# A four-layer float32 block: spectra of small kernels moved to the start, three PSUM banks for attention's first projections, and the scans' weights loaded ahead of a convolution

## The chip, the core and the metric

The kernel runs on one core of one Trainium2 chip, in float32 throughout. The metric is the device time of one execution in microseconds, the median of several runs. The engines are named as the profile names them: PE (TensorE), DVE (VectorE), ACT (ScalarE), POOL (GpSimd), and SP, which here only issues transfers. ACT can issue transfers too, on a queue of its own.

## The reference

The input `x` is an image of 256 x 256 positions with 128 channels (33.5 MB). Four layers follow each other; each one adds to its input a function of the group-normalised input:

```
x = x + L0(_gn(x))   # row attention: layer norm, q, k, v, g = 4 projections of 128 -> 128,
                     # softmax(q k / sqrt(32) + bias) v in 4 heads, per row of 256, gated, projected
x = x + L1(_gn(x))   # 128 -> 2 x 256, depthwise 3x3 convolution, silu, four selective scans
                     # (state 16) along rows and columns, forwards and backwards, gated, projected
x = x + L2(_gn(x))   # truncated Fourier mixing along both axes, then a two-layer MLP
x = x + L3(_gn(x))   # 16 steps of h = f * (A h) + inp, complex, with spectra A and B
```

`_gn` needs mean and variance of its whole input, so no layer can start before the one ahead of it is complete. In L3, A and B are the two-dimensional Fourier transforms, 256 x 256, of 7 x 7 kernels that are inputs of the program; they depend on no layer:

```
def _pad_and_fft(kr, ki, h, w, k):
    kern = kr + 1j * ki
    ph = (h - k) // 2
    pw = (w - k) // 2
    padded = jnp.pad(kern, ((0, 0), (ph, h - k - ph), (pw, w - k - pw)))
    return jnp.fft.fft2(padded, axes=(-2, -1))
```

In L1 the scans need, besides the convolution's output, four small weights: `x_proj_w`, `dt_w` with its bias, exp of `A_logs`, and `Ds`.

## The kernel before, in words

The image is kept as 128 channels (partitions) by 65536 positions and goes through DRAM between the stages: `x` to `x1` (layer 0), `x2p` and `x2` (layer 1), `x3` (layer 2), `out` (layer 3). `program()` at L1640 calls them in turn.

**Statistics.** `stream_stats` (L76) reads `x` in 32 loads of 1 MB, issued by SP into four buffers `xs_t`, and DVE makes `bn_stats` of four pieces of 512 positions of each. `group_norm_coef` (L52 to L72) then makes the scale and shift `ab` of the normalisation: `bn_aggr` (L60), two small matmuls, a square root on ACT (L70), a reciprocal. Later layers make their statistics while they write their outputs.

**Layer 0.** `layer0` loads `w_q` to `w_o`; `row_norm` (L102) loads three more constants and makes a layer norm in 32 blocks of 2048 positions: load x (`l0a_x`, four buffers), centre by a matmul (L141), square, variance by matmul, root, reciprocal, spread by matmul, scale, affine; it writes `z` and a bias of four rows. `attention` (L231) then goes through 32 blocks of 8 rows. A block needs 16 projections (`project`, L265): four pieces of 512 positions times k, q, v, g. Each is one matmul (four small ones for v, L272; else L277) into the PSUM tile `l0b_mm`, of which there is one buffer, and one evacuation out of it, by DVE for k and v (L275, L279), by ACT for q and g (L281, L283). The 16 projections of block 0 come first, before anything else is there to do; those of every later block are mixed into the units of the block before it. A unit is half a row's heads: scores (L291) with a running bias (L302), exponentials (L317), a division on POOL (L326), transposes into the two PSUM tiles `l0b_tp0` and `l0b_tp1`, the product with v, a gate, and an output projection once per two rows (also through `l0b_mm`).[...]

**Layer 1.** `conv_block` (L414) loads `l1a_win` and `l1a_taps` and multiplies them (L436), then goes through 16 blocks of 16 image rows and two halves of the 256 inner channels: x1 loaded (`l1a_xp`, L453), normalised on DVE (L457), projected (`l1a_pi`, L466), copied by ACT into `l1a_xi` (L473), the nine taps divided between PE, ACT, POOL and DVE, and a silu that writes both `l1a_o` and its transposed sibling `l1a_ot` (L530), stored to `l_xc` (L535, 1 MB) and `l_xct` (L539, 4 MB). Then `scan_weights` (L915) loads `xproj`, `dtw`, `alog` and `ds` on SP, makes exp of `alog` (L922), multiplies it by −1 (L923), and makes four diagonal matrices `dsum` out of the sum of `ds` (L926, L930). `scan_stream` goes through 4 directions of 128 chunks of 512 positions. A chunk's way is: block load `l1b_xc` (L641), xproj matmuls into `l1b_du` (L665), a copy to `l1b_xd` (L677), a store and broadcast loads of B and C (L679 to L691), the softplus of dt (L697 to L731), `l1b_du` and `l1b_db` (L739, L761), and per state the exponential `l1b_da` (L779) and the scan itself (L794) on DVE. `scan_end` merges the four directions.

**Layer 2** works through Fourier matrices on PE. **Layer 3** (`layer3`, L1383) begins with `kernel_spectra` (L1350): three loads, 8 accumulated pairs of matmuls (L1368 to L1372; the profile counts two instructions for each float32 matmul, 32), 32 evacuations into `l3k_o` on DVE (L1374 to L1377), and two stores of 1.79 MB into the DRAM tile `l_spec`. It then scales its weights (`wall`, `ball`, L1408 to L1416), loads a block of x (`l_x`) and 4 rows of `spec` (`l_tu`), makes the second half of the transform (`l_sps`, L1453) and the gates (`l_gp`, L1481), and runs the 16 steps on the whole block.

**What sets the order.** Within `row_norm`, `attention`, `conv_block`, `scan_stream` and `scan_end` the order of the instructions of each engine is written out by hand (`manual_schedule`); in layer 3 this holds for ACT alone. Elsewhere, and between these parts, the scheduler of the tile framework orders them by its own costs. Each engine, SP and ACT's queue included, carries out its stream in that order, and a wait at its head holds all behind it. SBUF comes from pools, which take over the room of pools that were closed before; the tile that is written there first waits for the last readers of what lay there.

Of the kernel before, what the change touches and what calls it, by code (L numbers as in the profile page):

```python
# [10 lines left out]
F32 = mybir.dt.float32  # L11
AF = mybir.ActivationFunctionType
ALU = mybir.AluOpType
AX = mybir.AxisListType
PSUM = bass.MemoryType.PSUM
DRAM = bass.MemoryType.DRAM

P = 128
S = 256
NPOS = S * S  # L20
CH = 512
# [21 lines left out]
        self.pool = pool  # L43


def load(nc, pool, src, name):
    to = pool.tile(list(src.shape), F32, name=name)
    nc.sync.dma_start(to, src)
    return to


# [179 lines left out]
def attention(c, x, x1, zs, bs, w, stats):  # L231
# [3 lines left out]
    tc, nc = c.tc, c.nc  # L235
# [4 lines left out]
    with ExitStack() as a:  # L240
        one = a.enter_context(tc.tile_pool(name="l0b_one", bufs=1))
        io = a.enter_context(tc.tile_pool(name="l0b_io", bufs=2))
        wk = a.enter_context(tc.tile_pool(name="l0b_wk", bufs=2))
        ps2 = a.enter_context(tc.tile_pool(name="l0b_p2", bufs=2, space=PSUM))
        ps1 = a.enter_context(tc.tile_pool(name="l0b_p1", bufs=1, space=PSUM))
# [19 lines left out]
        def project(b, i):  # L265
            k = blocks[b]
            j, n = i // 4, "kqvg"[i % 4]
            cs = bass.ts(j, CH)
            mm = ps1.tile([P, CH], F32, name="l0b_mm")
            if n == "v":  # L270
                for m in range(4):
                    nc.tensor.matmul(  # L272
                        mm[:, bass.ts(m, P)], k["z"][:, bass.ts(4 * j + m, P)], w["v"], start=True, stop=True
                    )
                nc.vector.tensor_copy(k["v"][:, 4 * j : 4 * j + 4].rearrange("p m o -> p (m o)"), mm)  # L275
                return
            nc.tensor.matmul(mm, w[n], k["z"][:, cs], start=True, stop=True)  # L277
            if n == "k":
                nc.vector.tensor_copy(k["k"][:, cs], mm)  # L279
            elif n == "q":  # L280
                nc.scalar.activation(k["q"][:, cs], mm, AF.Copy, scale=float(1.0 / np.sqrt(32)))  # L281
            else:
                nc.scalar.activation(k["g"][:, cs], mm, AF.Tanh, scale=0.5)  # L283
# [44 lines left out]
        def transposes(u):  # L328
            e = es.pop(u)
            for kt in range(2):  # L330
                tp = ps1.tile([P, 2, 2, P], F32, name=f"l0b_tp{kt}")
                for h in range(2):
                    for jt in range(2):
                        nc.tensor.transpose(tp[:, h, jt], e[:, 2 * h + jt, bass.ts(kt, P)], c.ident)
                at = ats[u, kt] = wk.tile([P, 2, S], F32, name=f"l0b_at{kt}")
                if kt == 0:
                    nc.scalar.copy(at, tp.rearrange("p h j q -> p h (j q)"))
                else:
                    nc.vector.tensor_copy(at, tp.rearrange("p h j q -> p h (j q)"))
# [44 lines left out]
        for i in range(UB):  # L384
            project(0, i)
# [3 lines left out]
        for u in range(N + 3):  # L389
            b, i = divmod(u, UB)  # L390
# [521 lines left out]
        y_out(N - 1, 1)  # L912


def scan_weights(c, pool):  # L915
    nc, t = c.nc, c.t
    w = {
        "xproj": load(nc, pool, t["l1_xproj"], "l1_xproj"),
        "dt": load(nc, pool, t["l1_dtw"], "l1_dtw"),
        "A": load(nc, pool, t["l1_alog"], "l1_A"),  # L920
    }
    nc.scalar.activation(w["A"], w["A"], AF.Exp)  # L922
    nc.vector.tensor_scalar(w["A"], w["A"], -1.0, None, ALU.mult)  # L923
    ds_ = load(nc, pool, t["l1_ds"], "l1_ds")
    both = pool.tile([P, 2, 2], F32, name="l1_both")
    nc.vector.tensor_tensor(both, ds_[:, 0:2], ds_[:, 2:4], ALU.add)  # L926
    w["dsum"] = pool.tile([P, 2, 2, P], F32, name="l1_dsum")
    for k in range(2):
        for dh in range(2):
            nc.vector.tensor_scalar(w["dsum"][:, k, dh], c.ident, both[:, k, dh : dh + 1], None, ALU.mult)  # L930
    return w


def scan_end(c, x1, ab, y02, y13, x2p, x2, stats):
# [412 lines left out]

def kernel_spectra(c, dram_t):  # L1350


    tc, nc, t = c.tc, c.nc, c.t
    with ExitStack() as a:
        one = a.enter_context(tc.tile_pool(name="l3k_one", bufs=1))
        wk = a.enter_context(tc.tile_pool(name="l3k_wk", bufs=2))
        ps = a.enter_context(tc.tile_pool(name="l3k_ps", bufs=2, space=PSUM))
# [3 lines left out]
        for ut in range(2):  # L1361
            us = bass.ts(ut, P)

            o = wk.tile([P, 2, 7, 2, 2, 64], F32, name="l3k_o")
            for q0, nq in ((0, 4), (4, 3)):
                qs = slice(q0, q0 + nq)
                re = ps.tile([P, nq, 2, 64], F32, name="l3k_re")
                nc.tensor.matmul(re, phase[:, 0, us], kr[:, qs], start=True, stop=False)  # L1368
                nc.tensor.matmul(re, phase[:, 1, us], ki[:, qs], start=False, stop=True)
                im = ps.tile([P, nq, 2, 64], F32, name="l3k_im")  # L1370
                nc.tensor.matmul(im, phase[:, 0, us], ki[:, qs], start=True, stop=False)
                nc.tensor.matmul(im, phase[:, 2, us], kr[:, qs], start=False, stop=True)  # L1372
                for ab_ in range(2):
# [4 lines left out]
            nc.sync.dma_start(  # L1378
                dram_t[us].rearrange("u r f -> u (r f)"), o.rearrange("u s q k r c -> u (s q k r c)")
            )  # L1380


def layer3(c, x3, out, ab):  # L1383

# [3 lines left out]
    tc, nc, t = c.tc, c.nc, c.t  # L1388
# [2 lines left out]
    NB = NPOS // BL  # L1391
    full, half = [P, NT, 2, 64], [P, NT, 64]
    with ExitStack() as a:
        dram = a.enter_context(tc.tile_pool(name="l3_dram", bufs=1, space=DRAM))
# [25 lines left out]
        phase = load(nc, one, t["c_phase_w"], "l3_phase")  # L1420
# [324 lines left out]
```

## Time and profile before

| what | us |
|---|---|
| runs of the kernel before: lowest, median, highest | 34311.81, 34312.65, 34319.6 |
| profiled execution, its own time | 34318.44 |
| its span in the trace | 34316.7 |
| first statistics (loads and bn_stats) | 7.7 to 87.6 |
| row norm, from the first centre matmul | 96.92 to about 545 |
| attention: projections of block 0 | 558.33 to 602.64 |
| attention, all | to 2919 |
| convolution, from its first load to the last store issued | 2926.5 to 3889.8 |
| scans: first wait for weights to the end of the last chunk | 3889.8 to about 29520 |
| merging of scans; layer 2 | to about 30600; to 32117 |
| layer 3 | 32117 to 34316.7 |

The times of the stages are read off the timeline of the profiled execution, in microseconds from the start of its span. Over the whole span PE is busy 85%, DVE 91%, ACT 66% and POOL 80%, and the mean clock granted to PE is 0.917 of the full one. A line of a timeline gives start, duration, engine, line and operation, output and input tiles, and in brackets the idle time just before it with what ended that. A line of the windows view gives, for a stretch of the span, the busy time and the number of instructions of each engine, the granted clock, the share of the 16 transfer engines that was busy, and the rate in GB/s.

### The profile page before, as it was taken

How to read it: one execution, taken by the hardware profiler on the slowest of the kernel's cores; microseconds unless marked ns; L12 is line 12 of the kernel's file. 1: busy time of each engine (PE TensorE's matmuls, PEld its weight loads, DVE VectorE, ACT ScalarE, POOL GpSimd, SP SyncE). 2: the span in 40 equal slices, each digit the busy share in tenths (PEclk: the TensorE clock that was granted, in tenths of full speed). 3: DMA queues.
4: the chain of work that ended last, by engine and by line, in shares of the span. 5: the costliest groups of instructions: out<-in, count | busy, mean ns of one | idle time of the engine just before them, and what ended most of it. 6: DMA issues, size and time to landing. Idle time of an engine off the chain costs nothing. (4 is left out here: it accounts for less than half of the span.)

```text
span 34316.7 us, 256885 instructions
## 1 busy us (share of the span) xinstructions
PE 29098.7 (85%) x72308; PEld 12172.7 (35%) x72308; DVE 31152.4 (91%) x23833; ACT 22759.1 (66%) x46957; POOL 27431.3 (80%) x6996
## 2 busy tenths in 40 slices
PE   7999888888888888888888888888888888899888
PEld 2554333333333333333333333333333333334444
DVE  5668999999999999999999999999999999863699
ACT  3667777777777777777677777777777777532476
POOL 2446799999999999999999999999999999620000
PEclk8999999999999999999999999999999999999888
DMA  3113455555555555555555555555555555674111
GB/s 137 45 42 119 186 190 191 189 191 192 191 190 191 191 190 191 191 191 189 196 201 203 201 202 199 202 201 202 201 201 200 201 202 203 211 235 144 64 34 33
DMA packets 2076531, 5947.89 MB, mean 173 GB/s; under 512 B 115207, under 2 KB 1379608, under 8 KB 1499222
## 3 DMA queue, kind: packets, MB, share of 16 engines
q1 hardware_dynamic: 1939926, 5864.32, 47.3%
q10 hardware_dynamic: 135168, 67.13, 0.7%
q8 instruction: 570, 9.34, 0.1%
q14 instruction: 867, 7.10, 0.1%
HBM read 5238.41 MB, written 692.58 MB: 173 GB/s over the span
## 5 line engine op out<-in xcount | busy, mean ns | idle before, releaser
L794 DVE TENSOR_TENSOR_SCAN l1b_h<-l1b_da,l1b_state,l1b_db 128x1024 f32<-128x1024 f32 x8192 | 18793.6, 2336 | 596.2 <-ACT l1b_db L783 585.3
L809 POOL TENSOR_TENSOR l1b_hc<-l1b_h,l1b_cc 128x2048 f32<-128x2048 f32 x4096 | 18444.4, 4527 | 329.9 <-DVE l1b_h L794 329.9
L828 PE MATMUL l1b_y<-l1b_hc,ident 128*128 128x512 f32 x32768 | 16054.5, 639 | 1108.4 <-POOL l1b_hc L809 1108.4
L779 ACT ACTIVATE l1b_da<-l1b_dl,l_A 128x512 f32<-128x512 f32 (+1 forms) x16384 | 11297.4, 690 | 3156.0 <-DVE l1b_h L794 2848.1
L828 PEld LDWEIGHTS l1b_y<-l1b_hc,ident 128*128 128x128 f32 x32768 | 6526.4, 205 | 10680.7 <-issue 8160.1
L761 POOL TENSOR_TENSOR l1b_db<-l1b_bb,l1b_dus 128x2048 f32<-128x2048 f32 x1536 | 6965.0, 4535 | 46.9 <-DMA l1b_bb<-l1b_bc 46.9
L761 DVE TENSOR_TENSOR l1b_db<-l1b_bb,l1b_du 128x2048 f32<-128x2048 f32 x2048 | 4658.6, 2275 | 35.2
L783 ACT ACTIVATE l1b_db<-l1b_state,l1b_db,l1b_af 128x1 f32<-128x1 f32 x8192 | 3045.1, 372 | 0.0
L697 PE MATMUL l1b_mm<-l1b_xd,l_dtw 41*128 41x512 f32 x2048 | 1373.4, 755 | 1694.3 <-ACT l1b_dus L750 1688.5
L723 PE MATMUL l1b_mm<-l1b_tail,ident 128*128 128x512 f32 x2048 | 1296.2, 719 | 1399.8 <-ACT l1b_tail L717 1397.3
L805 ACT COPY l1b_state<-l1b_h 128x4 f32<-128x4 f32 x4095 | 789.6, 193 | 2433.5 <-DVE l1b_h L794 2433.4
L326 POOL TENSOR_TENSOR l0b_e<-l0b_e,l0b_den 128x1024 f32<-128x1024 f32 x512 | 969.0, 1893 | 1403.2 <-DVE l0b_den L325 784.3
L723 PE MATMUL l1b_mm<-l1b_relu,ident 128*128 128x512 f32 x2048 | 1313.9, 730 | 0.0
L697 PEld LDWEIGHTS l1b_mm<-l1b_xd,l_dtw 41*128 41x128 f32 x2048 | 338.4, 206 | 2508.9 <-ACT l1b_dus L750 2111.6
L750 ACT COPY l1b_dus<-l1b_mm 128x512 f32<-128x512 f32 x512 | 299.6, 585 | 1388.6 <-DVE l1b_db L761 1388.1
L761 DVE TENSOR_TENSOR l1b_db<-l1b_bb,l1b_mm 128x2048 f32<-128x2048 f32 x512 | 1171.6, 2288 | 18.2 <-ACT l1b_dus L750 0.7
L302 DVE CUSTOM_DVE_ANT_0 l0b_e<-l0b_sc,l0b_bias 128x256 f32<-128x256 f32 x2048 | 745.4, 420 | 419.3 <-PE l0b_sc L291 416.0
L723 PEld LDWEIGHTS l1b_mm<-l1b_tail,ident 128*128 128x128 f32 x2048 | 376.8, 207 | 2070.6 <-ACT l1b_tail L717 1822.7
L317 ACT ACTIVATE l0b_e<-l0b_e,l0b_top 128x256 f32<-128x256 f32 x2048 | 1012.1, 498 | 1.9 <-DVE l0b_top L302 1.9
L665 PE MATMUL l1b_du<-l1b_xc,l_xproj 128*40 128x512 f32 x2048 | 981.6, 602 | 32.7 <-DMA l_xproj<-in_l_xproj 29.1
L731 ACT COPY l1b_dl<-l1b_mm 128x512 f32<-128x512 f32 x1024 | 587.4, 574 | 524.6 <-DVE l1b_du L739 517.2
L985 POOL TENSOR_TENSOR l1c_y<-l1c_y,l1c_yt 128x512 f32<-128x512 f32 x256 | 394.7, 1564 | 606.6 <-DMA l1c_y<-l_y 527.1
(261 smaller groups left out, 30140.8 us busy)
## 6 DMA issues: line engine op xcount, KB each, us to landing
l1b_bb<-l1b_bc SPq DMA_DIRECT2D x2048, 1024.0 KB
l1b_cc<-l1b_bc SPq DMA_DIRECT2D x2048, 1024.0 KB
l1b_xc<-l_xc SPq DMA_DIRECT2D x128, 1024.0 KB
l_y<-l1b_yo SPq DMA_DIRECT2D x128, 1024.0 KB
l1b_xc<-l_xct SPq DMA_DIRECT2D x256, 512.0 KB
l_y<-l1b_yo SPq DMA_DIRECT2D x256, 512.0 KB
l_xc<-l1a_o SPq DMA_DIRECT2D x64, 1024.0 KB
l_xct<-l1a_ot SPq DMA_DIRECT2D x16, 4096.0 KB
```

The costliest lines, as they stand in the source:

```text
L317: nc.scalar.activation(e[:, i], e[:, i], AF.Exp, scale=-1.0, bias=top[:, i : i + 1], accum_out=den[:, i : i + 1],)
L326: nc.gpsimd.tensor_tensor(e, e, den[:, :, None].to_broadcast([P, 4, S]), ALU.mult)
L665: nc.tensor.matmul(du1[:40], w["xproj"][:, dh, k, :], in_block(blocks[ch][0], ch, dh), start=dh == 0, stop=dh == 1,)
L697: nc.tensor.matmul(mm, w["dt"][:, chunks[ch][0], dh * P : dh * P + P], xds[ch % 3][0:41], start=True, stop=True,)
L723: nc.tensor.matmul(mm, c.ident, part, start=i == 0, stop=i == 1)
L761: eng.tensor_tensor(db, bbs[g // 2], du[:, None, :].to_broadcast([P, G, CH]), ALU.mult)
L779: nc.scalar.activation(da[:, o + lo : o + hi], dl[:, lo:hi], AF.Exp, scale=w["A"][:, k, dh, n : n + 1])
L783: nc.scalar.activation(first, states[k][:, dh, two : two + 1], AF.Identity, scale=af[:, two : two + 1], bias=first,)
L794: nc.vector.tensor_tensor_scan(h_, a_, d_, states[k][:, dh, one : one + 1], ALU.mult, ALU.add)
L805: nc.scalar.copy(states[k][:, dh, n0 : n0 + G], hs[g][:, :, 0 if k >= 2 else CH - 1])
L809: nc.gpsimd.tensor_tensor(hc, hs[g], ccs[g // 2], ALU.mult)
L828: nc.tensor.matmul(ys[j % 2], c.ident, hc[:, i], start=False, stop=j // 2 * G + i == 15)
```

## The change

There are three parts.

First, `kernel_spectra` is called in `program()` ahead of `stream_stats`, within one group of pools that is closed after both. Its three loads and its two stores are issued by ACT instead of SP, its 32 evacuations are made by ACT instead of DVE, and `spec` is a DRAM tile of the program.

Second, the 16 projections of attention's block 0 take in turn the PSUM tiles `l0b_mm`, `l0b_tp0` and `l0b_tp1`. The later blocks use `l0b_mm` as before. The transposes' tiles have their shape changed to suit both.

Third, the four weights of the scans are loaded before `conv_block` is called, issued by ACT; `scan_weights` keeps the arithmetic, and its place in the program's text.

In the built program the streams of the engines differ as follows. PE: the spectra's 16 matmuls stand at its start. ACT: three loads, 32 copies and two stores at its start; and, after the square root of layer 1's coefficients, the four weight loads, the table load and the exponential of `alog`, all ahead of the first copy into `l1a_xi`. DVE: the 32 copies are gone from layer 3, and the arithmetic on `ds` and on the exponential stands ahead of the multiplication of the taps. SP: the three loads and two stores of the spectra and the four weight loads are gone; two loads of x for the statistics wait for the completion of the two `spec` stores, since completions are counted on eight shared lanes; the row norm's first two loads of x stand ahead of `w_q` to `w_o`; at the convolution's start the two loads of `l1a_xp` wait for `xproj` and `dtw` on such lanes; and at its end the last stores of `l_xc` and `l_xct` stand ahead of the first two loads of `l1b_xc`, behind which they stood before. All other instructions keep their order on their engines.

```
-def load(nc, pool, src, name):
+def load(nc, pool, src, name, queue=None):
     to = pool.tile(list(src.shape), F32, name=name)
-    nc.sync.dma_start(to, src)
+    (queue or nc.sync).dma_start(to, src)
...
-            mm = ps1.tile([P, CH], F32, name="l0b_mm")
+            bank = ("mm", "tp0", "tp1")[i % 3] if b == 0 else "mm"
+            mm = ps1.tile([P, CH], F32, name=f"l0b_{bank}")
...
-                tp = ps1.tile([P, 2, 2, P], F32, name=f"l0b_tp{kt}")
+                tp = ps1.tile([P, CH], F32, name=f"l0b_tp{kt}")
+                tp = tp.rearrange("p (h j q) -> p h j q", h=2, j=2)
...
-def scan_weights(c, pool):
-    nc, t = c.nc, c.t
-    w = {
-        "xproj": load(nc, pool, t["l1_xproj"], "l1_xproj"),
-        "dt": load(nc, pool, t["l1_dtw"], "l1_dtw"),
-        "A": load(nc, pool, t["l1_alog"], "l1_A"),
-    }
+def scan_weights(c, pool, w):
+    nc = c.nc
+    w["A"], w["dt"], ds_ = w["alog"], w["dtw"], w["ds"]
     nc.scalar.activation(w["A"], w["A"], AF.Exp)
     nc.vector.tensor_scalar(w["A"], w["A"], -1.0, None, ALU.mult)
-    ds_ = load(nc, pool, t["l1_ds"], "l1_ds")
...
-        conv_block(c, x1, ab, xc, xct)
         with tc.tile_pool(name="l1_w", bufs=1) as wp:
+            w = {n: load(c.nc, wp, c.t[f"l1_{n}"], f"l1_{n}", c.nc.scalar) for n in ("xproj", "dtw", "alog", "ds")}
+            conv_block(c, x1, ab, xc, xct)
             tc.keep_in_program_order(c.nc.scalar.preload_act_table_set(EXP_LN))
-            w = scan_weights(c, wp)
+            scan_weights(c, wp, w)
...
-        kr = load(nc, one, t["l3_kr"], "l3k_kr")
-        ki = load(nc, one, t["l3_ki"], "l3k_ki")
-        phase = load(nc, one, t["c_phase_h"], "l3k_phase")
+    kr = load(nc, one, t["l3_kr"], "l3k_kr", nc.scalar)
+    ki = load(nc, one, t["l3_ki"], "l3k_ki", nc.scalar)
+    phase = load(nc, one, t["c_phase_h"], "l3k_phase", nc.scalar)
...
-                    nc.vector.tensor_copy(o[:, 0, qs, ab_, 0], re[:, :, ab_])
-                    nc.vector.tensor_copy(o[:, 0, qs, ab_, 1], im[:, :, ab_])
-                    nc.vector.tensor_copy(o[:, 1, qs, ab_, 0], im[:, :, ab_])
-                    nc.vector.tensor_scalar(o[:, 1, qs, ab_, 1], re[:, :, ab_], -1.0, None, ALU.mult)
-            nc.sync.dma_start(
+                nc.scalar.copy(o[:, 0, qs, ab_, 0], re[:, :, ab_])
+                nc.scalar.copy(o[:, 0, qs, ab_, 1], im[:, :, ab_])
+                nc.scalar.copy(o[:, 1, qs, ab_, 0], im[:, :, ab_])
+                nc.scalar.mul(o[:, 1, qs, ab_, 1], re[:, :, ab_], -1.0)
+        nc.scalar.dma_start(
...
-        spec = dram.tile([S, 14, 256], F32, name="l3_spec")
-        kernel_spectra(c, spec)
...
-        stream_stats(c, t["x"], c.stats[0])
+        spec = dram.tile([S, 14, 256], F32, name="l3_spec")
+        with ExitStack() as a:
+            kernel_spectra(c, spec, a)
+            stream_stats(c, t["x"], c.stats[0])
...
-        layer3(c, x3, out, group_norm_coef(c, c.stats[1], "3"))
+        layer3(c, x3, out, spec, group_norm_coef(c, c.stats[1], "3"))
```

More of the change, by code (lines that the diff above doesn't have):

```diff
@@ L930, in scan_weights @@
             nc.vector.tensor_scalar(w["dsum"][:, k, dh], c.ident, both[:, k, dh : dh + 1], None, ALU.mult)
-    return w
 def scan_end(c, x1, ab, y02, y13, x2p, x2, stats):
@@ L1344, in layer2, with kernel_spectra @@
                 nc.sync.dma_start(x3[:, sl], xo)
-def kernel_spectra(c, dram_t):
+def kernel_spectra(c, dram_t, a):
     tc, nc, t = c.tc, c.nc, c.t
[L1354 to L1357, printed above, removed]
-        kr = load(nc, one, t["l3_kr"], "l3k_kr")
-        ki = load(nc, one, t["l3_ki"], "l3k_ki")
-        phase = load(nc, one, t["c_phase_h"], "l3k_phase")
[L1361 to L1373, printed above, removed]
-                    nc.vector.tensor_copy(o[:, 0, qs, ab_, 0], re[:, :, ab_])
-                    nc.vector.tensor_copy(o[:, 0, qs, ab_, 1], im[:, :, ab_])
-                    nc.vector.tensor_copy(o[:, 1, qs, ab_, 0], im[:, :, ab_])
-                    nc.vector.tensor_scalar(o[:, 1, qs, ab_, 1], re[:, :, ab_], -1.0, None, ALU.mult)
-            nc.sync.dma_start(
-                dram_t[us].rearrange("u r f -> u (r f)"), o.rearrange("u s q k r c -> u (s q k r c)")
-            )
@@ L1383, in layer3 @@
-def layer3(c, x3, out, ab):
+    one = a.enter_context(tc.tile_pool(name="l3k_one", bufs=1))
+    wk = a.enter_context(tc.tile_pool(name="l3k_wk", bufs=2))
+    ps = a.enter_context(tc.tile_pool(name="l3k_ps", bufs=2, space=PSUM))
+    kr = load(nc, one, t["l3_kr"], "l3k_kr", nc.scalar)
+    ki = load(nc, one, t["l3_ki"], "l3k_ki", nc.scalar)
+    phase = load(nc, one, t["c_phase_h"], "l3k_phase", nc.scalar)
+    for ut in range(2):
+        us = bass.ts(ut, P)
+        o = wk.tile([P, 2, 7, 2, 2, 64], F32, name="l3k_o")
+        for q0, nq in ((0, 4), (4, 3)):
+            qs = slice(q0, q0 + nq)
+            re = ps.tile([P, nq, 2, 64], F32, name="l3k_re")
+            nc.tensor.matmul(re, phase[:, 0, us], kr[:, qs], start=True, stop=False)
+            nc.tensor.matmul(re, phase[:, 1, us], ki[:, qs], start=False, stop=True)
+            im = ps.tile([P, nq, 2, 64], F32, name="l3k_im")
+            nc.tensor.matmul(im, phase[:, 0, us], ki[:, qs], start=True, stop=False)
+            nc.tensor.matmul(im, phase[:, 2, us], kr[:, qs], start=False, stop=True)
+            for ab_ in range(2):
+                nc.scalar.copy(o[:, 0, qs, ab_, 0], re[:, :, ab_])
[3 more added lines that the diff above has]
+        nc.scalar.dma_start(
+            dram_t[us].rearrange("u r f -> u (r f)"), o.rearrange("u s q k r c -> u (s q k r c)")
+        )
@@ L1388, in layer3 @@
+def layer3(c, x3, out, spec, ab):
     tc, nc, t = c.tc, c.nc, c.t
@@ L1393, in layer3 @@
     with ExitStack() as a:
-        dram = a.enter_context(tc.tile_pool(name="l3_dram", bufs=1, space=DRAM))
         one = a.enter_context(tc.tile_pool(name="l3_one", bufs=1))
-        spec = dram.tile([S, 14, 256], F32, name="l3_spec")
-        kernel_spectra(c, spec)
         io = a.enter_context(tc.tile_pool(name="l3_io", bufs=3))
```

## The prediction

> **What bounds the kernel now.** I read the page's groups first, for the resource that sets the time, then the windows of the four places that the edits touch, then the timeline and the chain of waits there. The columns of a timeline line are start, duration, instruction, and in brackets the idle time before it and what ended it.
>
> ```profile
> L794 DVE TENSOR_TENSOR_SCAN l1b_h<-l1b_da,l1b_state,l1b_db 128x1024 f32<-128x1024 f32 x8192 | 18793.6, 2336 | 596.2 <-ACT l1b_db L783 585.3
> ```
> VectorE's scans are 18793.6 us of a span of 34316.7 and run from 3943 to about 29520 us. No edit touches their loop, so all that can change lies in what stands once, in series, ahead of them and after them: shares of some tens of us.
>
> ```profile
> 10.00:80.00 70.00, 0.00 (x0) 0.00 (x0) 69.30 (x113) 0.00 (x0) 0.00 (x0) 1.00 1.01 421
> 84.00:88.00 4.00, 0.00 (x0) 0.00 (x0) 3.96 (x7) 1.28 (x1) 0.00 (x0) 1.00 0.01 4
> 558.33:602.64 44.31, 33.10 (x57) 13.09 (x57) 5.54 (x8) 5.46 (x8) 0.00 (x0) 0.50 0.15 60
> 3905.00:3911.00 6.00, 3.23 (x4) 0.38 (x2) 0.00 (x0) 0.00 (x0) 0.00 (x0) 0.50 0.06 23
> 32128.70:32154.10 25.40, 24.21 (x32) 10.29 (x32) 10.28 (x32) 0.00 (x0) 0.00 (x0) 0.50 0.17 72
> ```
> Columns: busy time of PE, weight load, DVE, ACT, POOL, then granted clock, DMA share, GB/s. First statistics: transfers (1.01) and VectorE (69.30 of 70) are both full, and the transfers are done by 84. Projections: TensorE busy 33.1 of 44.3 us at half clock. Start of the scans: nothing but a transfer at 23 GB/s. Spectra: TensorE alone, at half clock.
>
> ```profile
> 597.12 0.60 ACT L281 ACTIVATE l0b_q<-l0b_mm 128x512 f32<-128x512 f32 x1 [5.02 <-PE l0b_mm L277]
> 597.77 2.07 PE L272 MATMUL l0b_mm<-l_wv,l0b_z 128*128 128x128 f32 x8 [0.69 <-ACT l0b_q L281]
> 599.88 0.69 DVE L275 COPY l0b_v<-l0b_mm 128x512 f32<-128x512 f32 x1 [4.93 <-PE l0b_mm L272]
> 600.63 2.08 PE L277 MATMUL l0b_mm<-l0b_z,l_wg 128*128 128x512 f32 x2 [0.79 <-DVE l0b_v L275]
> ...
> 3889.79 0.33 SPq L539 DMA_DIRECT2D l_xct<-l1a_ot  x1
> 3904.63 3.61 PE L665 MATMUL l1b_du<-l1b_xc,l_xproj 128*40 128x512 f32 x4 [29.08 <-DMA l_xproj<-in_l_xproj]
> 3911.03 0.31 ACT L922 ACTIVATE l_A<-l_A 128x128 f32<-128x128 f32 x1 [19.96 <-DMA l_A<-in_l_alog]
> 3911.24 0.56 ACT L677 COPY l1b_xd<-l1b_du 40x512 f32<-40x512 f32 x1
> ```
> Matmul and evacuation alternate through the one bank `l0b_mm`; the scans' first chunk waits for two weight loads that were issued behind a 4 MB store of `l_xct`.
>
> ```profile
> 32128.68 2.04 PE l3k_re L1368 x2
> ...
> 32154.12 5.70 DMA l_spec<-l3k_o
> 32160.02 3.88 DMA l_x<-x
> ```
> The chain in layer 3 runs through the spectra's matmuls (32 records), a store and the first x load behind it.
>
> [...]a pass over 512 columns takes 0.856 us cold, 0.43 warm; the conv warmed 4.8 us after its first matmul (2939.11 to 2943.9), the row norm after 3.7.[...] `dtw` has 41 rows[...]; its 168 KB between 3905 and 3911 are the 0.06 share and 23 GB/s above.[...]
>
> **A. Spectra beside the statistics, what it adds.** Two stores of `spec`, 1.79 MB each, and three small loads: 3.67 MB, at the best rate seen (434 GB/s, 8 to 10 us) 8.45 us, in a stage whose transfers are full. Slack: VectorE needs the last block at 85.06 and it landed at 84.0, 1.1 us; VectorE is faster than a block's transfer by 0.08 us (2.497 us against 2.58 at 406 GB/s), some 2 us over the rest of the stage. So the statistics end 8.45 − 1.1 − 2 = about 5.1 us later than 87.56. The 16 matmuls and 32 evacuations cost nothing: TensorE and ScalarE are idle in this window. SP, two of whose loads wait until the stores have landed (completion lanes are shared), may add to that; four buffers of 2.5 us cover it. Back again: the row norm's first matmul, at 96.92, had waited 2.64 us for its x load; in the changed order two x loads stand ahead of the weights and are there by 90. Net **+2.5 us**; bounds −2.5 (all hidden) and +5.
>
> **B. Projections over three banks.** Sixteen in 44.31 us, 2.77 each, are matmul 2.07, evacuation 0.60 to 0.69 and two handoffs. With three banks the evacuation of one lies beside the next matmuls, and TensorE runs without a gap: 2 × 0.856 = 1.71 us each cold, 16 × 1.71 = 27.4; that is the floor of the gain, 16.9 us. [...]after some 5 us cold (three projections) 13 × 0.856 = 11.1, sum 16.2, a gain of 28.1. Evacuations at 0.6 to 0.69 alternate over two engines, so they keep up with 0.856. Then the scores start warm, where before the clock stayed at half until 622.85; that stretch holds 17.2 us of PE work, but it is a fill in which each step waits on other engines (PE busy 17.2 of 20.2), and it may go cold again. I take 3.5 of a possible 1 to 6. **−31.6 us**; bounds −17 and −35. The tp banks are first used for transposes after scores that follow the last projection, so nothing new waits there.
>
> **C. Weights loaded ahead of the convolution, what it adds.** In the new order ScalarE's stream has the four DMAs, the table load and exp(`alog`) ahead of its first `l1a_xi` copies, and VectorE's has the products of `ds` and −exp(A) ahead of the multiplication of the taps (L436, 2.56 us at 2934.07) and the two normalisations of the conv's input (1.35 and 1.61 us). Both engines work in order, so the conv's start waits for `alog` to land. `alog` shares the queue with `dtw`, which took 6 us alone on one engine and here meets the taps and x loads: I put its landing at 2940, from 2936.5 (alone) to 2942. After it: exp 0.31, ×−1 0.23, dsum 0.88, taps 2.56, and the two normalisations 2.96: the second ends at about 2947.3 where it ended at 2942.6. ScalarE's copies wait no longer than the matmuls do, and TensorE's cold stretch comes as much later. That is 4.7 us, and about 1.1 for the taps' own transfer, which shares the engines with four more: **+5.8 us**; bounds +1 and +10.
>
> **D. Start of the scans, what it removes.** The waits for `xproj` (3904.63) and `alog` (3911.03) go. What is late next: in the new order SP issues the last `l_xct` store (4 MB, issue 3889.79) ahead of the scans' first `l1b_xc` load, which stood before it, at 3876.74. The store's data run until about 3902.6 (`xproj`, queued behind it, landed at 3904.6), then 1 MB at the 300 GB/s of such loads is 3.4 us: 3906, and the copy of `l1b_xd` at 3906 + 1.75 + 0.5 = 3908.3 instead of 3911.24. **−2.9 us**; bounds −6 and 0. Had the load kept its place, the whole 15 us would have gone.
>
> **E. Layer 3, what it removes.** `l_ball` is there at 32124.5. Before: `l_sps`, which opens the loop, began at 32166.08. After: three loads fewer and no store on SP, so x is issued at about 32126.8 and with its 3.88 us is there at 32130.7; the shift's matmuls and the scaled weights (32131.0) and two gp matmuls (2.05) put `l_sps` at 32133.1. **−32.9 us**; bounds −30 and −36. The store of `spec` is long done.
>
> **Sum.** 2.5 − 31.6 + 5.8 − 2.9 − 32.9 = −59.1. The profiled execution took 34318.44 us (span 34316.7), which gives 34259.3; it stands 5.8 above the median of the runs, 34312.65, from which the forecast is 34312.65 − 59.1 = 34253.5, **34254**. This is 0.17%. I take 0.2% (68.6 us: 34244 and 34381) as about what a measurement of this kernel can tell from no change.
>
> **Rivals.**
> 1. Everything hides: statistics −2 (the x loads' head start counts, the stores don't), projections −35, conv +1, scans −6, layer 3 −36: −78, 34235; with one or two of these only, some 34240. For it: four x buffers, three free engines. Against: a DMA share of 1.01, and VectorE's new order. Chance of passing −68.6: 0.2.
> 2. The clock stays cold in the projections (−17), or the conv waits for its upper bound (+10): −40 to −45, about 34270. For it: TensorE stayed at half clock for 44 us with a busy share of 75%. Chance 0.16.
> 3. Slower:[...] Its centre matmuls come at 146.55, 160.20, 173.86, 187.51, a period of 13.65[...].[...] Against: [...]the three runs agree within 8 us. Chance 0.02.
> 4. The weights' early load brings nothing (the 4 MB store decides): it is the sum's D at 0 with C at +5.8, and lies in the forecast's range, 34257.
>
> **Numbers.** Forecast with rival 4: 0.62; rivals 1, 2, 3: 0.2, 0.16, 0.02. The range goes from rival 1's single parts, 34238, to rival 2 with both, 34276. Faster by over 0.2%: 0.2; within: 0.79; slower: 0.01.
>
> **What would show it.** A: the last bn_stats ends near 92.7, the first centre matmul is near 99.4. B: projections in about 16 us with the clock at 1.00 from the third or fourth on; 27 us and 0.50 would be rival 2. C: the taps' multiplication on VectorE waits for `l_A`, and the first `l1a_xi` copy comes near 2948 after allowing for A and B. D: the first `l1b_du` matmul waits for `l1b_xc`, no weight. E: `l_sps` 9 us after `ab`. Wrong would be a new wait inside the scans or the attention's steady state: nothing is moved there, so each would have to keep its length to within some us.

## The result, and the profile after

The changed kernel takes 34256.26 us (median of 20 runs, 34247.13 to 34261.2) where the kernel before takes 34312.65 (20 runs beside it, 34299.25 to 34319.6): 56.4 us less, a ratio of 0.9984 with a 95% interval of [0.9978, 0.999]. The forecast was 34254. The profiled execution of the changed kernel has a span of 34249.9, that of before 34316.7, so the two traces are 66.8 apart, 10 more than the medians; where those 10 come from is told below the table.

Each row is a stretch between two marks that both traces have; the third column of numbers is the difference.

| stretch, from mark to mark | before | after | difference | forecast |
|---|---|---|---|---|
| start to bn_aggr (L60): first statistics | 87.60 | 97.88 | +10.3 | +5.1 |
| to the first centre matmul (L141) | 9.32 | 6.72 | −2.6 | −2.6 |
| row norm, to the first projection | 461.41 | 462.23 | +0.8 | 0 |
| 16 projections, to the first scores | 44.31 | 16.74 | −27.6 | −28.1 |
| attention, to layer 1's square root (L70) | 2323.37 | 2320.48 | −2.9 | −3.5 |
| to the first copy into `l1a_xi`, then to the last silu | 963.76 | 968.64 | +4.9 | +5.8 |
| to the first scan | 53.38 | 50.34 | −3.0 | −2.9 |
| all scans, to the first step of their merging | 25604.47 | 25605.12 | +0.7 | 0 |
| merging, to layer 2's square root | 1058.25 | 1045.37 | −12.9 | 0 |
| layer 2, to layer 3's square root | 1517.45 | 1516.99 | −0.5 | 0 |
| to the first `l_sps` | 42.69 | 9.41 | −33.3 | −32.9 |
| rest of layer 3 | 2150.69 | 2149.98 | −0.7 | 0 |

The stretches that the change touches come to −54.2, close to the −56.4 of the medians. Of the +4.9 of the convolution, 4.1 lie at its start, up to the first copy into `l1a_xi` (16.75 to 20.88 us after the square root); the rest is spread over 948 us and is not told from chance. The 12.9 of the merging belong to no edit: its instructions and their order are the same in both kernels, and in the profiles of the twelve runs below and of these two it took from 1039.7 to 1058.3 us, the kernel before at the upper end. One profile against one profile would have credited the change with it.

The windows view of the kernel after; the stretches answer to those shown of before (first statistics in two parts, projections, the scores' start, start of the scans, layer 3's way to `l_sps`):

```profile
10.00:50.00 40.00, 18.45 (x26) 7.97 (x24) 28.63 (x49) 9.43 (x31) 0.00 (x0) 1.00 1.01 408
50.00:90.00 40.00, 0.00 (x0) 0.00 (x0) 39.66 (x65) 0.00 (x0) 0.00 (x0) 1.00 1.01 420
566.83:583.57 16.74, 16.74 (x57) 9.62 (x57) 5.53 (x8) 5.46 (x8) 0.00 (x0) 0.84 0.36 148
583.57:603.78 20.21, 15.66 (x107) 10.19 (x106) 12.11 (x58) 13.67 (x48) 8.44 (x5) 0.83 0.00 0
3885.00:3889.00 4.00, 0.00 (x0) 0.00 (x0) 0.00 (x0) 0.00 (x0) 0.00 (x0) 0.50 0.85 321
32091.16:32099.99 8.83, 3.91 (x5) 0.69 (x5) 1.99 (x7) 0.91 (x1) 0.00 (x0) 0.50 0.67 202
```

In the 40 us of the first line VectorE is busy 28.63 instead of nearly all, though the transfers stay full: that is the loss. (The clock's 1.00 in the first two lines means nothing: the trace has no record of the clock before 108 us, and the spectra's matmuls over 512 columns follow each other at 0.85 us, as those in layer 3 of the kernel before do at 0.50.) In the projections TensorE is busy 16.74 of 16.74, and the mean clock of 0.84 says that some 5 us were cold (0.5) and the rest warm. The scans' start still waits for a transfer, now at 321 GB/s: a large one, not the 23 GB/s of `dtw`.

VectorE's timeline in the first statistics of the kernel after:

```profile
7.24 12.46 DVE L83 BATCH_NORM_STATS2 stats<-xs_t 128x6 f32<-128x512 f32 x20 [6.25 <-DMA xs_t<-in_x]
28.53 0.09 DVE L119 MEMSET l_wb<- 128x32 f32 x1 [8.84 <-PE l3k_im L1369]
28.53 9.55 DVE L83 BATCH_NORM_STATS2 stats<-xs_t 128x6 f32<-128x512 f32 x16
39.52 7.46 DVE L83 BATCH_NORM_STATS2 stats<-xs_t 128x6 f32<-128x512 f32 x12 [1.44 <-DMA xs_t<-in_x]
47.96 49.89 DVE L83 BATCH_NORM_STATS2 stats<-xs_t 128x6 f32<-128x512 f32 x80 [0.97 <-DMA xs_t<-in_x]
```

Three idle times, 11.25 us together. The longest stands ahead of a clearing of `l_wb`, a tile of the row norm that lies in the spectra's room and so waits for their last matmul.

The timeline at the start of the convolution, at the start of the scans, and the chain in layer 3, of the kernel after:

```profile
2917.27 0.31 ACT L920 ACTIVATE l_alog<-l_alog 128x128 f32<-128x128 f32 x1 [9.88 <-DMA l_alog<-in_l_alog]
2918.88 2.55 DVE L438 TENSOR_TENSOR l1a_taps<-l1a_taps,l1a_win 128x2304 f32<-128x2304 f32 x1
2924.93 0.58 ACT L475 COPY l1a_xi<-l1a_pi 128x512 f32<-128x512 f32 x1 [7.34 <-PE l1a_pi L468]
...
3872.71 0.32 SPq L541 DMA_DIRECT2D l_xct<-l1a_ot  x1
3873.20 2.43 SPq L643 DMA_DIRECT2D l1b_xc<-l_xc  x2
3889.83 3.61 PE L667 MATMUL l1b_du<-l1b_xc,l_xproj 128*40 128x512 f32 x4 [31.37 <-DMA l1b_xc<-l_xc]
```
```profile
32093.85 3.96 DMA l_x<-x
...
32099.99 7.12 PE l_sps L1447 x16
```

This is as forecast: VectorE multiplies the taps only after the weights' arithmetic; the first matmul of the scans waits for `l1b_xc`, which is issued 0.5 us behind the 4 MB store; in layer 3 only the load of x is left.

### The profile page after: what moved, and what is told of

Its sections match the earlier page's. It is cut to its first block, busy times and chain, and to the rows that moved or that the text cites. A ratio compares the mean times of both kernels' runs of the same rounds, so it can differ in the third digit from the quotient of the medians.

```text
span 34249.9 us, 256893 instructions
## 1 busy us (share of the span) xinstructions
PE 29062.3 (85%) x72308; PEld 12164.1 (36%) x72308; DVE 31137.1 (91%) x23801; ACT 22770.2 (66%) x46991; POOL 27433.4 (80%) x6996
## 5 line engine op out<-in xcount | busy, mean ns | idle before, releaser
L781 ACT ACTIVATE l1b_da<-l1b_dl,l_alog 128x512 f32<-128x512 f32 (+1 forms) x16384 | 11297.5, 690 | 3156.6 <-DVE l1b_h L796 2848.7
```

What stands on the lines that cost most here:

```text
L781: nc.scalar.activation(da[:, o + lo : o + hi], dl[:, lo:hi], AF.Exp, scale=w["A"][:, k, dh, n : n + 1])
```

## The experiments

Medians are given as the difference to the runs of the kernel before that were made beside them: 34314.04 for `p1_spectra`, `p2_banks`, `p3_weights` and `two_banks`, 34311.88 for `a_memset`, `c_late`, `d_room` and `all_three`, 34307.52 for `s_stall`, `s_late`, `c_split` and `best`. The interval of such a ratio is about ±0.0008 of it, ±27 us; so the totals tell the parts of the change from each other only roughly, and the stretches of the profiles decide.

**The three parts alone.** `p1_spectra`, the kernel before with the spectra moved only:

```
+            kernel_spectra(c, spec, a)
             stream_stats(c, t["x"], c.stats[0])
```

> The kernel before with the first part alone (spectra beside the statistics). Theory, part by part sum: statistics end near 97.9 as in the changed kernel, first centre matmul +7.7, layer 3's way from its coefficients to the first l_sps −33; together −25, about 34287. Rival, that layer 3's saving is partly given back later because its first blocks arrive before ACT is ready: −15 or less, over 34297.

−26.8 us (34287.28; 0.9992 [0.9984, 1.0]). bn_aggr at 97.84, first centre matmul at 104.55, `l_sps` 9.44 after the square root. The rest of layer 3 takes 2150.5 us, as before, so nothing of the saving is given back there.

`p2_banks`, the kernel before with the banks only:

```
+            bank = ("mm", "tp0", "tp1")[i % 3] if b == 0 else "mm"
+            mm = ps1.tile([P, CH], F32, name=f"l0b_{bank}")
```

> The kernel before with the second part alone (three banks for the first projections). Theory: projections 16.7 us instead of 44.3 with the clock at full from the third on, the attention's rest 2.9 shorter since it starts warm; −30.5, about 34282. Rival[...]: projections near 27 us, −17, about 34296.

−32.7 us (34281.33; 0.9991 [0.9983, 0.9999]). The window of its projections:

```profile
558.95:575.98 17.03, 17.03 (x56) 9.62 (x57) 5.54 (x8) 5.46 (x8) 0.00 (x0) 0.82 0.38 156
```

The same picture at another time in the run, so the warm clock is no accident. In all ten profiles with three banks the projections took 16.7 to 17.0 us, in the three with one bank 44.3 each time.

`p3_weights`, the kernel before with the weights' loads moved only:

```
+            w = {n: load(c.nc, wp, c.t[f"l1_{n}"], f"l1_{n}", c.nc.scalar) for n in ("xproj", "dtw", "alog", "ds")}
             conv_block(c, x1, ab, xc, xct)
```

> The kernel before with the third part alone (weights loaded ahead of the convolution). Theory: the convolution's first part is 4.9 us later, the scans' start 3.0 earlier: +1.9, about 34314, not to be told from before. Rival, that the early load of weights is worth its whole wait of 15 us: −10, about 34303.

+2.1 us (34316.12; 1.0 [0.9992, 1.0009]), no difference. The first copy into `l1a_xi` comes 21.58 us after the square root instead of 16.75, the first scan 50.1 after the last silu instead of 53.4. The three parts come to −57.4, the whole change to −56.4: as far as totals with such intervals can tell, they add up. The third part's two stretches, +4.8 and −3.2, leave nothing that can be seen.

**How many banks.** `two_banks`, the changed kernel:

```
-            bank = ("mm", "tp0", "tp1")[i % 3] if b == 0 else "mm"
+            bank = ("mm", "tp0")[i % 2] if b == 0 else "mm"
```

> The changed kernel with two banks instead of three for the first projections. Theory[...]: a bank's turn is 1.02 + 0.69 + two handoffs of 0.1 = 1.9 us for two projections, so 0.95 each against 0.87: the projections take about 18 us at full clock, 34258. Rival (the third bank is needed to warm): projections over 25 us at half clock, 34265 or more.

Projections 17.83 us, −52.5 in all (34261.55). Three lines of its timeline, two turns of TensorE and an evacuation beside them, and the window of the scores' start:

```profile
578.17 1.02 PE L278 MATMUL l0b_tp<-l0b_z,l_wq 128*128 128x512 f32 x2
578.37 0.69 DVE L280 COPY l0b_k<-l0b_mm 128x512 f32<-128x512 f32 x1 [1.22 <-PE l0b_mm L278]
579.12 1.16 PE L273 MATMUL l0b_mm<-l_wv,l0b_z 128*128 128x128 f32 x8
```
```profile
584.92:605.13 20.21, 16.22 (x89) 10.23 (x88) 10.07 (x48) 12.31 (x44) 7.54 (x4) 0.66 0.00 0
```

One overlap is what matters: in the projections the second bank gives 26.5 of the 27.6 us, the third the remaining 1.1, since a bank's turn of matmul, evacuation and handoffs (1.9 us, in which two projections are made) is a little longer than two warm matmuls (2 × 0.86 us). In the scores' start, which follows, the one profile with two banks is colder (0.66 instead of 0.83), and its attention takes 2322.8 us, only 0.6 less than before.

**The statistics' delay.** `a_memset`, the changed kernel with `l_wb` in room of its own:

```
-        wb = one.tile([P, 32], F32, name="l0_wb")
-        nc.vector.memset(wb, 0.0)
+        wb = c.wb
```

`c.wb` is a tile of the shared pool that is cleared at the start.

> The changed kernel with l0_wb in room of its own and cleared at the start, so that VectorE's clearing of it no longer waits for the spectra's last matmul. Theory (of the 10.3 us by which the statistics end later, the spectra's 3.7 MB of transfers make 5 to 7, VectorE's 8.84 us wait the rest): bn_aggr starts near 93 to 95 instead of 97.9, 34252. Rival (transfers alone set the end, VectorE only waits somewhere else): 97 to 98, 34256.

bn_aggr at 96.61, only 1.3 earlier; −55.1 in all (34256.81). The theory of two causes that add up fell. VectorE's timeline of this run:

```profile
7.09 14.91 DVE L85 BATCH_NORM_STATS2 stats<-xs_t 128x6 f32<-128x512 f32 x24 [6.06 <-DMA xs_t<-in_x]
24.00 2.47 DVE L85 BATCH_NORM_STATS2 stats<-xs_t 128x6 f32<-128x512 f32 x4 [1.99 <-DMA xs_t<-in_x]
29.88 4.93 DVE L85 BATCH_NORM_STATS2 stats<-xs_t 128x6 f32<-128x512 f32 x8 [3.41 <-DMA xs_t<-in_x]
...
46.79 49.71 DVE L85 BATCH_NORM_STATS2 stats<-xs_t 128x6 f32<-128x512 f32 x80 [0.32 <-DMA xs_t<-in_x]
```

The one wait for a matmul has become five waits for transfers (two of them, 1.64 and 2.59 us, are left out here), 9.95 us in all instead of 11.25. One rival is that SP's order costs the time, not the bytes: SP waited 3.2 us in this run for a store of `l_spec` to land before it issued a load of x. But in every window of 5 us from 5 to 95 us the transfers' share was 0.99 or more, so there was nothing left to be won by issuing earlier. To see each cause without the other, the stores were taken out of the stage: `s_stall`, and with `l_wb` moved too, `s_late`:

```
             stream_stats(c, t["x"], c.stats[0])
+            for there, o in os_:
+                c.nc.sync.dma_start(there, o)
```

> As the run with the late stores, but l0_wb lies in the spectra's room as in the change, so VectorE's clearing still waits for the spectra's last matmul. Theory (in the changed kernel that wait of 8.8 us lay over the wait for transfers, which is why its removal alone gave 1.3): with the stores gone it is bare, bn_aggr starts near 96. Rival (the clearing's wait is made of the transfers' delay and goes with it): below 90.

> The changed kernel with the two stores of the spectra issued by SP behind the last load of the statistics, and l0_wb in room of its own, cleared at the start. Theory (VectorE is at 99% in this stage, so each wait for a transfer is lost for good, and the stores' 3.7 MB are that wait): bn_aggr starts at 87.5 to 88.5 as in the kernel before; the row norm's constants and first x then queue behind the stores, so its first centre matmul comes near 100 instead of 104.6; 34252. Rival (the small loads and the order of the start are the cost, not the stores): bn_aggr over 93.

`s_stall` (34258.04, one run): bn_aggr at 96.42, with the 8.70 us of the clearing bare. `s_late`: bn_aggr at 87.72, as in the kernel before. So the two waits each cost about 8.8 us alone and 10.2 together: they lay over each other. The clearing in `s_stall`, and then VectorE and the row norm's start in `s_late`:

```profile
28.56 0.09 DVE L119 MEMSET l_wb<- 128x32 f32 x1 [8.70 <-PE l3k_im L1370]
```
```profile
8.12 79.50 DVE L85 BATCH_NORM_STATS2 stats<-xs_t 128x6 f32<-128x512 f32 x128 [7.08 <-DMA xs_t<-in_x]
87.72 3.62 DVE L62 BATCH_NORM_AGGREGATE gn_mv<-stats 128x2 f32<-128x768 f32 x1
99.14 0.29 DVE L128 TENSOR_SCALAR l_scaled<-l_cent,ab 128x128 f32<-128x128 f32 x1 [4.03 <-DMA l_cent<-in_c_cent]
```

In time nothing is won: the first centre matmul comes at 104.17 (104.60 in the changed kernel), −55.0 in all (34252.52). The stores, behind which the expectation saw the row norm's constants and first x, are through by 92 us (the transfers' share is 0.07 from 92 to 94 and 0.01 from 94 to 96). What holds these loads is the order of SP: in this build the five weights `w_q` to `w_o`, which the changed kernel issues behind the first x, stand ahead of `l_cent`, and SP waits 16.1 us, until `ab` is made, before it issues the first of them. SP's wait in `s_late` (us in total, times, longest), and two of its issues:

```profile
SPq L50 <- DVE ab L74: 16.1, 1, 16.1
```
```profile
94.94 0.33 SPq L50 DMA_DIRECT2D l_wq<-in_l_wq  x1
97.21 0.43 SPq L50 DMA_DIRECT2D l_cent<-in_c_cent  x1
```

The first x follows at 99.1. A build with late stores and the old order of SP was not tried.

**The convolution's start.** `c_late`, the changed kernel with the weights' arithmetic held behind the convolution:

```
-    nc.scalar.activation(w["A"], w["A"], AF.Exp)
+    keep(nc.scalar.activation(w["A"], w["A"], AF.Exp))
```

`keep` holds an instruction in the order of the program; the products on VectorE are held in the same way.

> The changed kernel with the arithmetic on the scans' weights held behind the convolution, their loads as early as in the change. Theory (VectorE's and ScalarE's wait for the weights is what delays the convolution): from layer 1's square root to the first copy into l1a_xi 16.8 to 17.5 us instead of 20.9; nothing lost at the scans' start, which waits for l1b_xc: 34252. Rival (the loads' share of the engines delays taps and x, whoever waits): 20 us or more as before the edit, 34256.

20.59 us from square root to first copy, 20.88 in the changed kernel; −57.0 in all (34254.84). The rival holds: VectorE's wait had only moved from the weights to x, of which the first block takes two loads. `c_split`, the changed kernel with `dtw` loaded in 32 and 9 rows:

```
+            c.nc.scalar.dma_start(dtw[0:32], c.t["l1_dtw"][0:32])
+            c.nc.scalar.dma_start(dtw[32:41], c.t["l1_dtw"][32:41])
```

> The changed kernel with the 41 rows of dtw loaded as 32 and 9 rows. Theory (dtw on a single transfer engine holds up that engine's part of everything behind it, the convolution's first x too): from layer 1's square root to the first copy into l1a_xi 17 to 18 us instead of 20.9, 34252. Rival (SP's wait on shared completion lanes, or the sheer number of loads): 20 or more.

17.65 us; −55.3 in all (34252.22), where 3 us can't be seen. Timeline of the x loads' reader in `c_late` (its first line merges four issues, of which the second is shown by itself, with SP's wait ahead of it), and then in `c_split` with the exponential of `alog`:

```profile
2908.51 16.60 SPq L455 DMA_DIRECT2D l1a_xp<-x  x4
2919.01 1.35 DVE L459 TENSOR_SCALAR l1a_xp<-l1a_xp,ab 128x2048 f32<-128x2048 f32 x1 [8.48 <-DMA l1a_xp<-x]
2922.31 1.61 DVE L459 TENSOR_SCALAR l1a_xp<-l1a_xp,ab 128x2304 f32<-128x2304 f32 x1 [1.95 <-DMA l1a_xp<-x]
```
```profile
2916.53 0.38 SPq L455 DMA_DIRECT2D l1a_xp<-x  x1
```
```profile
SPq L455 <- DMA l_dtw<-in_l_dtw: 7.6, 1, 7.6
```
```profile
2909.01 12.21 SPq L455 DMA_DIRECT2D l1a_xp<-x  x4
2909.13 0.31 ACT L920 ACTIVATE l_alog<-l_alog 128x128 f32<-128x128 f32 x1 [2.69 <-DMA l_alog<-in_l_alog]
2914.52 1.35 DVE L459 TENSOR_SCALAR l1a_xp<-l1a_xp,ab 128x2048 f32<-128x2048 f32 x1 [1.48 <-DMA l1a_xp<-x]
```

From the issue of the first x load to its use it is 10.5 us with `dtw` in one piece, 5.5 with two; `alog` is used 4.9 us after its issue (at 2904.28) instead of 12.0 in the changed kernel. In `c_late`, between 2913 and 2917, next to nothing is moved:

```profile
2913.00:2917.00 4.00, 0.00 (x0) 0.00 (x0) 0.00 (x0) 0.00 (x0) 0.00 (x0) 0.50 0.11 35
```

For most of this stretch it is 22 to 25 GB/s, the rate of `dtw` alone in the kernel before (23 at a share of 0.06). That fits a first x load whose other parts are done and whose last one stands behind `dtw`: its use at 2919.01 is 2.5 us after SP saw `dtw` land, and if each of the 16 engines carries an even part of its 1 MB, that part takes 2.7 us at 24 GB/s (an estimate). `c_split` bears it out for this load and for `alog`, which are both on their way before `dtw` lands. The 22 to 25 GB/s agree with one engine: a sixteenth of the 421 GB/s of the full first stage is 26, and in the kernel after the share from 2914 to 2917 is 0.07, at 25 GB/s. That its 41 rows are what leaves `dtw` to one engine was not shown. What the runs do show is that such a load, issued by ACT, holds up the loads around it, SP's among them: 10.5 us against 5.5 for the first x load.

The second x load has another reason to be late, and it is this load that the first copy waits for: SP issues it only at 2916.53, since it stands on the completion lane of `dtw` and SP waits 7.6 us for that (the traces of the kernels before and after count all landings on eight semaphores). In `c_split` this wait is 0.2 us, and the second load is issued at 2909.43, right behind the first, and used at 2918.41. The rival that the expectation of `c_split` named, SP's wait on the lanes, is therefore not excluded: the edit removed both, and how much of the 3 us belongs to each stays open.

**The scans' start.** `d_room`, the changed kernel with two tiles of 2 KB per partition ahead of the chunk buffers:

```
         st = a.enter_context(tc.tile_pool(name="l1b_st", bufs=1))
+        sf = a.enter_context(tc.tile_pool(name="l1b_sf", bufs=1))
         io = a.enter_context(tc.tile_pool(name="l1b_io", bufs=2))
```

Why this edit: by the addresses of the built program, which no trace shows, the first `l1b_xc` buffer lies at the same place in both kernels, but the weights' pool, opened earlier, pushes the convolution's tiles 8 KB up. The buffer lay over `l1a_xp` before, which is free early, and after the change over `l1a_each`, which POOL and DVE read up to the last row; with 4 KB ahead of it, it lies over `l1a_xp` again. The run shows that moving the buffers restores the order of SP; that it is this tile which matters is read from the addresses alone.

> The changed kernel with two small tiles of the scans (tail, relu) placed ahead of the chunk buffers, so that these no longer lie over the convolution's per-channel weights, and the first chunk loads stand ahead of the last 4 MB store again. Theory: the copy into l1b_xd comes about 1.5 us after the convolution's last silu instead of 20.9; what is late next is the broadcast loads behind the store, so the first scan comes some 38 us after it instead of 50.3: −12, 34244. Rival (the 4 MB store holds up everything behind it alike): 48 to 50, 34255.

−75.5 us (34236.4; 0.9978 [0.997, 0.9987]). First scan 36.3 us after the last silu instead of 50.3. Its timeline:

```profile
3870.78 0.33 SPq L541 DMA_DIRECT2D l_xct<-l1a_ot  x1
3870.81 3.55 PE L668 MATMUL l1b_du<-l1b_xc,l_xproj 128*40 128x512 f32 x4 [14.24 <-ACT l1a_ot L532]
3874.53 0.58 ACT L680 COPY l1b_xd<-l1b_du 40x512 f32<-40x512 f32 x1 [2.46 <-PE l1b_du L668]
3888.78 2.29 DVE L764 TENSOR_TENSOR l1b_db<-l1b_bb,l1b_mm 128x2048 f32<-128x2048 f32 x1 [3.57 <-DMA l1b_bb<-l1b_bc]
```

The copy came 3.8 us after the silu, not 1.5: I had left out the first chunk's matmuls, which start only when the convolution is done. What is late next is the broadcast load `l1b_bb` behind the store, as expected: SP waits 5.4 us for the store to land before it issues the first of these loads at 3883.79. The stretch is 14.0 us shorter than in the changed kernel, the total about 19; the difference is within the interval.

**Versions of several edits.** `all_three` is `a_memset`, `c_late` and `d_room` together:

> The changed kernel with the three edits (clearing, arithmetic late, chunk loads early) together. Theory: they lie in different stages and add up, −4 −4 −12 = −20, 34236. Rival (the stages share room and queues, so that one edit spoils another): over 34246.

−70.7 us (34241.22; 0.998 [0.9972, 0.9988]), five less than expected: the gain of `d_room` and nothing that the totals show beside it. `best` is `d_room`, `c_split` and `s_late`:

> The changed kernel with the chunk buffers moved, dtw in two loads, the spectra's stores late and l0_wb in room of its own. Theory: −14 to −20 (chunk loads, as measured), −3.5 and −4: 34256 − 24 = about 34231, and faster than both kernels. Rival (what is saved early is waited for later): 34240 or more.

−75.3 us (34232.2; 0.9978 [0.9969, 0.9987]): faster than the kernel before by 0.22%, 19 more than the 56.4 of the change, where 24 were expected. From `d_room` alone (−75.5) it can't be told; in its profile the convolution's start is 17.52 and the scans' start 36.0 us, but the first centre matmul comes at 103.83, so late stores bring nothing here either.

## Why the prediction was right, and where it wasn't

**B and E, right in mechanism and size.** −27.6 for −28.1 with the warm clock from the third or fourth projection, −2.9 for −3.5 in the attention behind them, from its first 40 us, the scores' start, which did go partly cold again (clock 0.83, where it was 0.51 before), −33.3 for −32.9 in layer 3. Rival 2, the cold clock, would have been 27 us; no run showed it. The scores' start in the kernel before, to set beside the window after:

```profile
602.64:622.85 20.21, 17.16 (x81) 10.63 (x80) 9.68 (x47) 11.85 (x43) 7.23 (x4) 0.51 0.00 1
```

That TensorE warms when its matmuls leave no gaps was the author's estimate; for these matmuls it held in all eleven profiles with two or three banks (a mean clock of 0.84 in the kernel after, 0.82 in `p2_banks`, 0.84 in `two_banks`). It isn't general: in the spectra of the kernel before, TensorE is busy 24.21 of 25.40 us and stays at 0.50 throughout, as the prediction's own window shows. Those matmuls read 7 partitions instead of 128; whether that is the reason, no run shows.

**D, right in its cause; the size was luck.** The forecast read in the order of SP that the store now stands ahead of the chunk load, and put the gain at 2.9 instead of 15; the first matmul does wait for that load, and `d_room`, which restores the order, gets 14 more. But the way to 2.9 was wrong. The copy into `l1b_xd` was to come 18.5 us after the last silu, where it was 21.5 before; it came at 20.9:

```profile
3893.61 0.58 ACT L679 COPY l1b_xd<-l1b_du 40x512 f32<-40x512 f32 x1 [19.62 <-PE l1b_du L667]
```

The first matmul began 17.1 us after the silu instead of 16.2, and the chunk's matmuls took 3.61 us where the forecast put 1.75, although its own line at 3904.63 shows 3.61 (the window it calls "nothing but a transfer" holds them too). So 0.6 of the 3.0 came as forecast, and the rest depends on where the clock warmed: 20.8 us after the silu in this profile, 25 to 26 in those that took 52.5 to 52.8. The eight profiles with this order took 50.1 to 53.9 us, 51.6 in the mean, the three with the old one 53.0: a gain of 1.4. Rival 4, D at nothing, is not told from this by any total.

**C, right in sign and size, half right in its cause.** +4.9 for +5.8, or 4.1 at the convolution's start, of which the forecast spoke. It had `alog` land at 2940, shifted by the 22 us that A and B gave 2918; it landed at 2917.27. But the step "the conv's start waits for `alog` to land" isn't the whole: without that wait (`c_late`) x itself is as late, held by the same `dtw` in two ways: its first load on the transfer engine, its second because SP doesn't issue it before `dtw` has landed. The forecast named the single engine and didn't carry it on to x, and it left out SP's wait of 7.2 us in this profile, though the lanes are named in the text on the change.

**A, the step that failed.** +7.7 for +2.5 at the centre matmul, outside the part's own bounds of −2.5 and +5, and +10.3 for +5.1 at the end of the statistics. The term is "8.45 − 1.1 − 2" (which is 5.35, not 5.1): both subtractions were wrong. The 2 us came from a VectorE that is faster than the transfers, 2.497 us for a block against 2.58 at 406 GB/s; but the prediction's own window has 421 GB/s, which is 2.49 us a block. VectorE is as full as the transfers, so its waits aren't made up: after the last of them it runs 49.89 us without a pause, at the same 2.49 us a block. And the slack of 1.1 us is that of the last block, while the stores come in the first third, when the blocks land just in time. What is left is the stores' own time: 8.9 us between `s_late` and `a_memset` (96.61 − 87.72), against 8.45 from 434 GB/s. That the stores are issued by ACT and the loads by SP changed nothing: they shared one bandwidth (408 GB/s from 10 to 50 us with the stores among the loads, 421 from 10 to 80 us for the loads alone before). The other 1.3 are from "the 16 matmuls … cost nothing": they hide, but a clearing on VectorE waits for the last of them. The forecasts of no loss from SP's wait for the stores ("four buffers … cover it"), and the −2.6 for the x loads that go first, were right.

**The total** was 2.8 us off the median. The five parts' errors were +5.2 (A), +1.1 (B), −0.9 (C), −0.1 (D) and −0.4 (E), 4.9 together, less than the spread of the runs (34247.13 to 34261.2). That it landed so near is in part luck: A's error alone is 5.2, and D's size is one profile's. Two small slips beside these: rival 2 "with both" sums to 34272, not 34276, and by the clock's own records the row norm warmed 3.3 and the convolution 4.4 us after its first matmul, not 3.7 and 4.8.

Rival 3, a slower row norm, didn't occur: it took 459.6 to 462.9 us in all fourteen profiles. Why the merging varies by 18 us from one execution to the next was not tried.

## What to carry to other kernels

In a stage where transfers and the reading engine are both full, look for the whole transfer time of added bytes (here 8.9 us for two stores), and for waits that hide each other: taking away one of two showed 1.3 us here, each alone was worth 8.8. A load that moves earlier must be followed on its transfer engine and on its completion lane too: here a load beside it took 10.5 us instead of 5.5, and another was not issued for 7.6 us, until it had landed. A rebuild can reorder the issuing queues, as `s_late` shows, and a pool that is opened earlier shifts the addresses of all that follow, so that buffers may wait for other tiles than before. Look first at which stretch of the trace differs and whether an edit touches it; a stretch that no edit touches shows how much one profile is worth.

## What the runs showed that was not expected

A TensorE that alternates with its evacuation at 75% busy stays at half clock for all 44 us, three times out of three, and two banks are enough to make it warm; yet one that is busy 95% of the time with matmuls over 7 partitions stays cold too. Two loads instead of one for 41 rows shortened a neighbouring load from 10.5 to 5.5 us. A tile of 16 KB in all, cleared on VectorE, held the statistics for 8.8 us, and its removal was worth 1.3.
